# Four graph layers on one core: from layer-by-layer jobs to five lanes with a planned order for every engine

## The chip, the core and the metric

The kernel runs on one core of a Trainium2 chip. The metric is device microseconds (us) for one execution; a comparison runs both kernels in turns on the same chip. Engines are TensorE (PE; its weight loads are listed apart as PEld), VectorE (DVE), ScalarE (ACT), GpSimd (POOL) and SyncE (SP, which issues most loads and all stores).

## The reference, cut

```python
# x: (64, 256, 128) fp32, adj: (256, 256), 0/1; four layers, each with a residual and a layernorm
x = layernorm(x + L0(x, adj, ...))   # h = x@wo; e[i,k] = leaky(u1[idx1]+u2[idx2]) masked by adj;
                                     # softmax over i (the rows); out = att @ h + x @ wself
x = layernorm(x + L1(x, adj, ...))   # h = x@W; e[i,j] = leaky(h_i.a_src + h_j.a_dst) masked by adj + I;
                                     # softmax over j; elu(att @ h)
x = layernorm(x + L2(x, adj, ...))   # five gated steps:
                                     #   m = adj@h;  z, r = sigmoid(..m.. + u3 h);  v = tanh(..m.. + u5 (r*h))
                                     #   h = (1-z)*h + z*v
x = layernorm(x + L3(x, adj, ...))   # x W0 + adj x W1 + adj^2 x W2 + adj^3 x W3 (both halves share adj)
```

The graphs are independent. Both kernels work in 32 **units** of two graphs, 512 nodes of 128 features each.

## The kernel before

Everything is fp32. A unit's layer is a generator whose `yield`s cut it into pieces; four generators are live, and one piece of each is given out in turn. The program hands each engine its instructions as one list, so this turn-taking is the order of every engine's queue. The jobs are layer-major: all 32 units go through layer 0, then all through layer 1, and so on.

```python
    def run(jobs, width, gap):
        live, wait = [], 0
        while jobs or live:
            if jobs and len(live) < width and wait <= 0:
                live.append(jobs.pop(0))
                wait = gap
            wait -= 1
            live = [j for j in live if next(j, StopIteration) is not StopIteration]

    jobs = [layer(u) for layer in (layer0, layer1, layer2, layer3) for u in range(NU)]
    run(jobs, 4, 1)
```

Layer 1's attention has queries on partitions: mask added, leaky, maximum, exp with sums, then p is transposed for the product with h.

```python
    def layer1(u):
        ...
        for g in range(G):
            b, c = g // NC, g % NC
            nc.vector.scalar_tensor_tensor(e[:, b, c, :], ps_e[:, b * N : (b + 1) * N], es[:, g : g + 1], neg1[:, c, :],
                                           op0=ALU.add, op1=ALU.add)
        leaky(e, 0.2)
        nm = buf("nm", 4, [P, G])
        nc.vector.tensor_reduce(nm, e.rearrange("p b c j -> p (b c) j"), AX.X, ALU.max, negate=True)
        ...
            nc.scalar.activation(p[:, g // NC, g % NC, :], e[:, g // NC, g % NC, :], AF.Exp,
                                 bias=nm[:, g : g + 1], accum_out=s[:, g : g + 1])
        ...
                    nc.tensor.transpose(ps_t[:, jc, ic * P : (ic + 1) * P], p[:, b, ic, jc * P : (jc + 1) * P], ident)
            nc.vector.tensor_copy(pT[:, b], ps_t)
```

A normalisation takes four `bn_stats` and four `bn_aggr` a unit; layer 2 uses real sigmoids for r and z.

Of the kernel before, what the change touches and what calls it, by code (L numbers as in the profile page):

```python
# [8 lines left out]
F32 = mybir.dt.float32  # L9
AF = mybir.ActivationFunctionType  # L10
# [3 lines left out]
P = 128  # L14
NEG = -1.0e30
EPS = 1e-5
STEPS = 5


@with_exitstack  # L20
def kernel(
# [34 lines left out]
    G = UB * NC  # L56

    const = ctx.enter_context(tc.tile_pool(name="const", bufs=1))
    work = ctx.enter_context(tc.tile_pool(name="work", bufs=2))
    psum = ctx.enter_context(tc.tile_pool(name="psum", bufs=8, space=bass.MemoryType.PSUM))  # L60

    def bank(shape):
        return psum.tile(shape, F32, tag="ps", name="ps")


    def load(name, src, shape, eng=nc.gpsimd):
        t = const.tile(shape, F32, tag=name, name=name)
        eng.dma_start(t, src)
        return t
# [3 lines left out]
    X = []  # L73

    def load_x(u):
        X.append(load(f"x{u}", x_u[u], [P, UB, NC, D], nc.sync))

    load_x(0)
    adj_t = load("adj_t", adj.rearrange("(c p) j -> p c j", p=P), [P, NC, N], nc.sync)
    for u in range(1, NU):  # L80
        load_x(u)

    wo = load("wo", others_weight, [D, D])
    att = const.tile([D, 2], F32, tag="att", name="att")
    for k in range(2):
        nc.gpsimd.dma_start(att[:, k : k + 1], att_weight[k * D : (k + 1) * D, :])
    wself = load("wself", self_weight, [D, D])
    w1 = load("w1", W, [D, D])
    asd = const.tile([D, 2], F32, tag="asd", name="asd")
    nc.gpsimd.dma_start(asd[:, 0:1], a_src)  # L90
    nc.gpsimd.dma_start(asd[:, 1:2], a_dst)
    gates = [load(f"gate{k}", w, [D, 2, D]) for k, w in enumerate(
        w.rearrange("o (s d) -> o s d", s=2) for w in (w3_w, w4_w, w5_w))]
    u3 = load("u3", u3_w, [D, D])
    u5 = load("u5", u5_w, [D, D])
    biases = const.tile([D, 5], F32, tag="biases", name="biases")
    for k, b in enumerate((w3_b, w4_b, w5_b, u3_b, u5_b)):
        nc.gpsimd.dma_start(biases[:, k : k + 1], b.rearrange("(p o) -> p o", o=1))
    wk = load("wk", weight_1, [D, D, 7])


    ident = const.tile([P, P], F32, tag="ident", name="ident")
    make_identity(nc, ident)
    nhalf = const.tile([P, G], F32, tag="nhalf", name="nhalf")
    nc.vector.memset(nhalf, -0.5)

    def transposed(name, src):
        ps = bank([P, P])
        nc.tensor.transpose(ps, src, ident)
        t = const.tile([P, P], F32, tag=name, name=name)  # L110
        nc.vector.tensor_copy(t, ps)
        return t

    adjT = const.tile([P, NC, N], F32, tag="adjT", name="adjT")
    for mc in range(NC):
        ps = bank([P, N])
        for ic in range(NC):
            nc.tensor.transpose(ps[:, ic * P : (ic + 1) * P], adj_t[:, ic, mc * P : (mc + 1) * P], ident)
        nc.vector.tensor_copy(adjT[:, mc, :], ps)

    neg0 = const.tile([P, NC, N], F32, tag="neg0", name="neg0")
    nc.vector.tensor_scalar(neg0, adjT, 0.0, NEG, op0=ALU.is_le, op1=ALU.mult)
    neg1 = const.tile([P, NC, N], F32, tag="neg1", name="neg1")
    nc.vector.tensor_copy(neg1, adj_t)
    for c in range(NC):
        nc.vector.tensor_add(neg1[:, c, c * P : (c + 1) * P], adj_t[:, c, c * P : (c + 1) * P], ident)
    nc.vector.tensor_scalar(neg1, neg1, 0.0, NEG, op0=ALU.is_le, op1=ALU.mult)

    def projected(name, w, vecs):
        wT = transposed(name + "T", w)  # L130
        ps = bank([P, 2])
        nc.tensor.matmul(ps, wT, vecs, start=True, stop=True)
        t = const.tile([P, 2], F32, tag=name, name=name)
        nc.vector.tensor_copy(t, ps)
        return t

    wu = projected("wu", wo, att)
    wc = const.tile([P, 1], F32, tag="wc", name="wc")
    nc.vector.tensor_add(wc, wu[:, 0:1], wu[:, 1:2])
    wc_b = const.tile([P, P], F32, tag="wc_b", name="wc_b")  # L140
    nc.vector.tensor_copy(wc_b, wc.to_broadcast([P, P]))
    wsd = projected("wsd", w1, asd)
    wd_b = const.tile([P, P], F32, tag="wd_b", name="wd_b")
    nc.vector.tensor_copy(wd_b, wsd[:, 1:2].to_broadcast([P, P]))

    def layer2_weights():
        ws = []
        for k in range(3):
            ws.append(const.tile([D, D], F32, tag=f"gs{k}", name=f"gs{k}"))
            nc.vector.tensor_add(ws[k], gates[k][:, 0, :], gates[k][:, 1, :])  # L150

        nc.vector.tensor_sub(ws[0], ws[0], ws[1])
        wT = [transposed(f"gT{k}", ws[k]) for k in range(3)]
        bs = const.tile([D, 3], F32, tag="bs", name="bs")
        for k, j in enumerate((3, 3, 4)):
            nc.vector.tensor_add(bs[:, k : k + 1], biases[:, k : k + 1], biases[:, j : j + 1])
        return wT, transposed("u3T", u3), transposed("u5T", u5), bs

    def layer3_weights():

        w3 = const.tile([D, 2, 2, D], F32, tag="w3", name="w3")

        nc.vector.tensor_add(w3[:, 0, 0, :], wk[:, :, 0], ident)
        for k in range(1, 4):
            nc.vector.tensor_add(w3[:, k % 2, k // 2, :], wk[:, :, k], wk[:, :, k + 3])
        return w3

    def adj_squared():

        a2T = const.tile([P, NC, N], F32, tag="a2T", name="a2T")  # L170
        for mc in range(NC):
            ps = bank([P, N])
            for kc in range(NC):
                nc.tensor.matmul(ps, adj_t[:, kc, mc * P : (mc + 1) * P], adjT[:, kc, :],
                                 start=(kc == 0), stop=(kc == NC - 1))
            nc.vector.tensor_copy(a2T[:, mc, :], ps)
        return a2T

    (dT, wT4, wT5), u3T, u5T, bias2 = layer2_weights()
    w3 = layer3_weights()  # L180
    a2T = adj_squared()



    def buf(tag, bufs=2, shape=None):
        return work.tile(shape or [P, UB, NC, D], F32, tag=tag, name=tag, bufs=bufs)

    def feature_major(u):
        ps = bank([P, T])
        for g in range(G):  # L190
            nc.tensor.transpose(ps[:, g * P : (g + 1) * P], X[u][:, g // NC, g % NC, :], ident)
        xT = buf("xT", 6, [P, UB, N])
        nc.scalar.copy(xT.rearrange("p b n -> p (b n)"), ps)
        return xT

    def layernorm(u, y):

        st = buf("st", 4, [P, G, 6])
        mv = buf("mv", 4, [P, G, 2])
        for g in range(G):  # L200
            nc.vector.bn_stats(st[:, g, :], y[:, g, :])  # L201
        for g in range(G):
            nc.vector.bn_aggr(mv[:, g, :], st[:, g, :])
        ve = buf("ve", 4, [P, G])
        nc.vector.tensor_scalar_add(ve, mv[:, :, 1], EPS)  # L205
        rstd = buf("rstd", 4, [P, G])
        nc.gpsimd.tensor_tensor(rstd, ve, nhalf, op=ALU.pow)  # L207
        yield
        for g in range(G):
            nc.vector.tensor_scalar(X[u][:, g // NC, g % NC, :], y[:, g, :], mv[:, g, 0:1], rstd[:, g : g + 1],  # L210
                                    op0=ALU.subtract, op1=ALU.mult)

    def residual(u, other):

        y = buf("y", 4, [P, G, D])
        nc.vector.tensor_add(y, other, X[u].rearrange("p b c d -> p (b c) d"))
        return y

    def flat(t):
        return t.rearrange("p a b -> p (a b)")  # L220

    def leaky(e, slope):

        e = e.rearrange("p b c n -> p (b c n)")
        nc.vector.scalar_tensor_tensor(e, e, slope, e, op0=ALU.mult, op1=ALU.max)  # L225


    def layer0(u):
        xT = feature_major(u)
        yield  # L230
        ps_c = bank([P, T])
        nc.tensor.matmul(ps_c, wc_b, flat(xT), start=True, stop=True)
        ps_d = bank([P, UB])
        for b in range(UB):
            for k in range(2):
                nc.tensor.matmul(ps_d[:, b : b + 1], xT[:, b, k : N : 2], wu[:, k : k + 1],
                                 start=(k == 0), stop=(k == 1))
        ps_h = bank([P, G, D])
        for g in range(G):
            nc.tensor.matmul(ps_h[:, g, :], xT[:, g // NC, (g % NC) * P : (g % NC + 1) * P], wo,  # L240
                             start=True, stop=True)
        d = buf("d", 4, [P, UB])
        nc.vector.tensor_copy(d, ps_d)
        e = buf("e", 2, [P, UB, NC, N])
# [208 lines left out]
```

## Time and profile before

| | before |
|---|---|
| median of 3 runs | 2171.63 us (2171.27 to 2172.13) |
| profiled span, mean granted clock | 2168.6 us, 0.934 |
| TensorE, VectorE, ScalarE busy | 84%, 54%, 38% |

The page's busy shares are means over four layers with different limits. The prediction below shows the slices, the table of stages and the waits, and takes from the dense stretches what TensorE needs at full rate. One row that it names in words is this group (line, engine, operation, tiles, shapes, count; busy us and mean ns; idle before, and who ended it):

```profile
L365 DVE TENSOR_TENSOR t<-t,xT 128x512 f32<-128x512 f32 x160 | 110.3, 690 | 459.1 <-ACT t L363 459.1
```

VectorE waits there 459 us in all for layer 2's tanh. The prediction reads from it that the order of the queues, not the work in them, sets the pace of layer 2.

### The profile page before, as it was taken

The page shows a single profiled execution, that of the slowest core. Times are in us where ns is not written, and L with a number is a line of the kernel's source. Part 1 is how long each engine was busy: PE and PEld are TensorE (multiplying, and loading weights), DVE is VectorE, ACT ScalarE, POOL GpSimd, SP SyncE. Part 2 cuts the span into 40 slices and gives each one's busy share as a digit, 9 for nine tenths or more (in the row PEclk, how much of TensorE's full clock was granted, in tenths as well). Part 3 has the DMA queues.
Part 4 walks back from the last instruction along what each step waited for, and adds up shares of the span by engine and source line. Part 5 has one row for each costly group of instructions (what it writes and reads, how often), then busy time and mean ns, then how long its engine had stood idle before and what let it go on. Part 6 is the DMA issues. An engine that isn't in the chain of part 4 may idle for free.

```text
span 2168.6 us, 21458 instructions
## 1 busy us (share of the span) xinstructions
PE 1831.9 (84%) x7767; PEld 1247.7 (58%) x7767; DVE 1179.4 (54%) x3137; ACT 813.9 (38%) x1698; POOL 143.2 (7%) x152
## 2 busy tenths in 40 slices
PE   5888865556666998998998998998989989999998
PEld 4777754444444554555555555545545545568887
DVE  5988977777777535335335335354353353353333
ACT  1333333333333443443443443443434434433333
POOL 2111110000000000000000000000000000011111
PEclk9999977777777999999999999999999999999999
DMA  7000000000000000000000000000000000001111
GB/s 182 1 1 2 1 1 0 1 0 1 0 1 0 1 1 0 1 1 0 0 1 0 0 1 0 0 1 1 0 1 1 0 1 0 1 10 35 40 35 39
DMA packets 34842, 19.60 MB, mean 9 GB/s; under 512 B 1472, under 2 KB 34496, under 8 KB 34736
## 3 DMA queue, kind: packets, MB, share of 16 engines
q1 hardware_dynamic: 34064, 17.04, 2.9%
q8 instruction: 61, 1.00, 0.2%
q0 software_dynamic: 672, 1.19, 0.2%
q14 instruction: 45, 0.37, 0.1%
HBM read 9.84 MB, written 8.39 MB: 8 GB/s over the span
## 4 chain that ended last, share of the span: by engine, by line
PE 67%; DVE 20%; ACT 6%; POOL 3%; issue 2%; DMA 1%; POOLq 0%; ACTq 0%; DVEq 0%
PE ps L342 13%; PE ps L355 8%; PE ps L350 6%; PE ps L349 6%; PE ps L361 6%; PE ps L360 6%; PE ps L395 5%; ACT t L352 3%; PE ps L310 3%; DVE x L210 3%; DVE st L201 3%; POOL rstd L207 3%; PE ps L403 3%; PE ps L385 2%; DVE e L225 2%
## 5 line engine op out<-in xcount | busy, mean ns | idle before, releaser
L365 DVE TENSOR_TENSOR t<-t,xT 128x512 f32<-128x512 f32 x160 | 110.3, 690 | 459.1 <-ACT t L363 459.1
L342 PE MATMUL ps<-adjT,ht 128*128 128x256 f32 x1024 | 245.2, 382 | 25.8 <-ACT ht L375 25.8
L207 POOL TENSOR_TENSOR rstd<-ve,nhalf 128x4 f32<-128x4 f32 x128 | 132.7, 1037 | 2017.4 <-DVE ve L205 1881.1
L342 PEld LDWEIGHTS ps<-adjT,ht 128*128 128x128 f32 x1024 | 191.9, 190 | 99.2 <-ACT ht L375 56.4
L310 PE MATMUL ps<-ident,p 128*128 128x128 f32 x256 | 74.9, 422 | 166.0 <-ACT p L300 164.8
L355 PE MATMUL ps<-h,gT 128*128 128x512 f32 x320 | 180.1, 645 | 40.4 <-ACT t L352 40.4
L210 DVE TENSOR_SCALAR x<-y,mv,rstd 128x128 f32<-128x128 f32 x512 | 151.4, 344 | 92.7 <-POOL rstd L207 92.6
L354 DVE TENSOR_TENSOR y<-t,xT 128x512 f32<-128x512 f32 x160 | 110.0, 687 | 143.9 <-ACT t L352 143.9
L345 ACT COPY h<-ps 128x512 f32<-128x512 f32 x160 | 93.9, 587 | 225.9 <-PE ps L342 225.9
L201 DVE BATCH_NORM_STATS2 st<-y 128x6 f32<-128x128 f32 x512 | 115.9, 283 | 108.0 <-ACT y L407 107.2
L352 ACT ACTIVATE t<-ps,bs 128x512 f32<-128x512 f32 x160 | 110.0, 688 | 169.1 <-PE ps L350 169.1
L363 ACT ACTIVATE t<-ps,bs 128x512 f32<-128x512 f32 x160 | 110.1, 688 | 167.2 <-PE ps L361 167.2
L310 PEld LDWEIGHTS ps<-ident,p 128*128 128x128 f32 x256 | 48.7, 212 | 207.6 <-ACT p L300 180.9
L357 ACT ACTIVATE z<-ps,bs 128x512 f32<-128x512 f32 x160 | 110.0, 688 | 147.9 <-PE ps L355 147.9
L349 PE MATMUL ps<-xT,u3T 128*128 128x512 f32 x320 | 163.9, 594 | 0.0
L361 PE MATMUL ps<-y,u5T 128*128 128x512 f32 x320 | 163.5, 592 | 0.4 <-DVE y L354 0.4
L360 PE MATMUL ps<-h,gT 128*128 128x512 f32 x320 | 163.5, 592 | 0.0
L350 PE MATMUL ps<-h,gT 128*128 128x512 f32 x320 | 163.4, 592 | 0.0
L372 PEld LDWEIGHTS ps<-ident,xT 128*128 128x128 f32 x640 | 80.3, 144 | 112.5 <-issue 53.8
L372 PE MATMUL ps<-ident,xT 128*128 128x128 f32 x640 | 99.9, 280 | 35.5 <-DVE xT L368 35.5
L300 ACT ACTIVATE p<-e,nm 128x256 f32<-128x256 f32 x128 | 63.6, 499 | 161.0 <-DVE nm L296 161.0
L368 DVE TENSOR_TENSOR xT<-xT,t 128x512 f32<-128x512 f32 x160 | 110.5, 690 | 8.8
(124 smaller groups left out, 2954.5 us busy)
## 6 DMA issues: line engine op xcount, KB each, us to landing
x<-in_x_dram SPq DMA_DIRECT2D x32, 256.0 KB, 5.5
out_dram<-x SPq DMA_DIRECT2D x32, 256.0 KB, 2.3
wk<-in_L_gnn_weight_dram POOLq DMA_DIRECT2D x1, 448.0 KB, 6.6
gate<-in_L_gnn_w_w_dram POOLq DMA_DIRECT2D x3, 128.0 KB, 5.8
adj_t<-in_adj_dram SPq DMA_DIRECT2D x1, 256.0 KB, 3.2
u<-in_L_gnn_u_w_dram POOLq DMA_DIRECT2D x2, 64.0 KB, 5.9
wo<-L_gnn_others_weight_dram POOLq DMA_DIRECT2D x1, 64.0 KB, 3.4
wself<-n_L_gnn_self_weight_dram POOLq DMA_DIRECT2D x1, 64.0 KB, 5.2
```

Of the source, the lines that this page charges most:

```text
L201: nc.vector.bn_stats(st[:, g, :], y[:, g, :])
L207: nc.gpsimd.tensor_tensor(rstd, ve, nhalf, op=ALU.pow)
L210: nc.vector.tensor_scalar(X[u][:, g // NC, g % NC, :], y[:, g, :], mv[:, g, 0:1], rstd[:, g : g + 1], op0=ALU.subtract, op1=ALU.mult)
L310: nc.tensor.transpose(ps_t[:, jc, ic * P : (ic + 1) * P], p[:, b, ic, jc * P : (jc + 1) * P], ident)
L342: nc.tensor.matmul(ps_m[:, b, :], ht[:, b, mc, :], adjT[:, mc, :], start=(mc == 0), stop=(mc == NC - 1))
L349: nc.tensor.matmul(ps_r, u3T, hf, start=True, stop=False)
L350: nc.tensor.matmul(ps_r, wT4, mT, start=False, stop=True)
L352: nc.scalar.activation(r, ps_r, AF.Sigmoid, bias=bias2[:, 1:2])
L355: nc.tensor.matmul(ps_r, dT, mT, start=False, stop=True, skip_group_check=True)
L360: nc.tensor.matmul(ps_v, wT5, mT, start=True, stop=False)
L361: nc.tensor.matmul(ps_v, u5T, rh, start=False, stop=True)
L372: nc.tensor.transpose(ps_t[:, g, :], hT[:, g // NC, (g % NC) * P : (g % NC + 1) * P], ident)
```

## The change

Its intent is to keep TensorE full from start to end. Four things are new: (1) a **list plan**: the kernel is first written down as tasks with an engine, a cost in ns and the cells that they read and write; a plan then gives each engine its next ready task, oldest unit first, and fixes thereby the order of every queue and the use of the eight PSUM banks; (2) five **lanes**, each of which takes one unit through all four layers; (3) **layer 1's attention transposed**: keys on partitions, so no transposes of p, no maximum, the mask as a product, the row sums from a column of ones in h; (4) **paired statistics**: one `bn_stats` over two interleaved rows. Besides, sigmoids become tanh, layer 0's two weights (with the residual's identity) share one product, Prelu on ScalarE replaces VectorE's leaky passes, and all loads are issued by SyncE.

```diff
+LANES = 5
+LEAD = 20
+BANKS = 8
...
+class Plan:
+    LATENCY = {"pe": 220, "dve": 150, "act": 150, "pool": 200, "sp": 3000}
+    OWN = {"pe": 0, "dve": 70, "act": 70, "pool": 100, "sp": 0}
...
+    def seen_at(self, t, by):
+        return t.end if t.eng != by.eng else t.off + self.OWN[t.eng]
...
+            for e, tasks in ready.items():
+                if free[e] > now:
+                    continue
+                fit = [t for t in tasks if t.at <= now and len(t.takes) <= len(self.free_banks)]
+                if not fit:
+                    continue
+                t = min(fit, key=key)
...
+                free[e] = t.off = now + t.ns
+                t.end = t.off + self.LATENCY[e] + t.wait
...
 (layernorm)
-        for g in range(G):
-            nc.vector.bn_stats(st[:, g, :], y[:, g, :])
-        for g in range(G):
-            nc.vector.bn_aggr(mv[:, g, :], st[:, g, :])
+        for k, (c, view) in enumerate(pairs):
+            add(DVE, 330, lambda k=k, view=view: nc.vector.bn_stats(st.ap[:, k, :], view().rearrange("p j d -> p d j")),
+                (c,), (st,))
...
 (layer 1)
+            add(ACT, 400, lambda g=g, b=b: nc.scalar.activation(
+                e.ap[:, g, :], ps_e.ap[:, b * N : (b + 1) * N], AF.Prelu, bias=h.ap[:, g, D : D + 1], alpha=0.2),
+                (ps_e, h), (e,))
...
+        add(ACT, 950, lambda: nc.scalar.activation(ef, ef, AF.Exp), (e,), (e,))
+        add(DVE, 1150, lambda: nc.vector.tensor_mul(
+            p.ap.rearrange("p (b c) n -> p b (c n)", b=UB), e.ap.rearrange("p (b c) n -> p b (c n)", b=UB),
+            mask1.ap.rearrange("p (o c) n -> p o (c n)", o=1).to_broadcast([P, UB, NC * N])), (e, mask1), (p,))
...
 (layer 2)
-            nc.scalar.activation(r, ps_r, AF.Sigmoid, bias=bias2[:, 1:2])
+            add(ACT, 600, lambda ps_g=ps_g: nc.scalar.activation(r.ap, ps_g.ap, AF.Tanh, bias=bias2.ap[:, 1:2], scale=0.5),
+                (ps_g, bias2), (r,))
...
-    jobs = [layer(u) for layer in (layer0, layer1, layer2, layer3) for u in range(NU)]
-    run(jobs, 4, 1)
+    def spawn(u, lane):
+        for layer in (layer0, layer1, layer2, layer3):
+            layer(u, lanes[lane])
+
+    def first(t):
+        late = t.unit - (NU - LANES)
+        return (0, t.unit) if late < 0 else (1, t.step + late * LEAD)
+
+    with tc.manual_schedule():
+        for t in plan.run(spawn, range(NU), first):
+            t.fn()
```

LATENCY is the plan's **handover allowance**: how long after a task has left its engine another engine may count on its result; OWN is the same for the engine itself. `first` is the rule of what goes first: the oldest unit, and among the last five units the task with the fewest steps done, each unit LEAD (20) steps behind the one before.

## The prediction

> **What bounds the kernel now.** I read the page's busy shares first, then its forty slices, because a share over the whole span mixes stages.
>
> ```profile
> PE 1831.9 (84%) x7767; PEld 1247.7 (58%) x7767; DVE 1179.4 (54%) x3137; ACT 813.9 (38%) x1698; POOL 143.2 (7%) x152
> ...
> PE   5888865556666998998998998998989989999998
> ...
> DVE  5988977777777535335335335354353353353333
> ...
> PEclk9999977777777999999999999999999999999999
> ```
>
> The slices show four regimes. From slice 6 to slice 13 TensorE is 5 or 6 tenths busy, VectorE is at 7, and the granted clock sinks to 0.7; before and after that TensorE is at 8 or 9. The kernel runs layer after layer over all 32 units, so the regimes are the layers. From the TensorE timeline I took the times at which the first instructions of a new layer crowd out the last of the old (26, 262, 713 and 1928 us; the seams overlap by a few us) and asked for the busy time of each stretch. The columns are start:end, length, busy us and count of each engine, clock, share and rate of the DMA.
>
> ```profile
> 0.00:26.00 26.00, 4.81 (x18) 3.94 (x19) 7.36 (x31) 1.28 (x1) 10.46 (x24) 1.00 1.03 268
> 26.00:262.00 236.00, 204.17 (x1398) 177.03 (x1396) 208.08 (x664) 78.88 (x265) 28.52 (x28) 0.95 0.05 13
> 262.00:713.00 451.00, 276.81 (x1565) 229.90 (x1564) 349.31 (x910) 145.86 (x439) 35.15 (x34) 0.75 0.00 1
> 713.00:1928.00 1215.00, 1112.78 (x3654) 632.00 (x3653) 525.40 (x1105) 503.76 (x804) 35.76 (x33) 0.98 0.00 0
> 1928.00:2168.60 240.60, 233.28 (x1142) 204.82 (x1140) 89.27 (x430) 84.14 (x190) 33.27 (x33) 0.99 0.12 36
> ```
>
> So set-up takes 26 us, layer 0 236, layer 1 451, layer 2 1215, layer 3 241. Layer 1 is a chain and no full engine: its waits (who waited, for whom, us in total, times, longest) are those of the softmax, handed on from VectorE to ScalarE to TensorE.
>
> ```profile
> PEld ps L310 <- ACT p L300: 180.9, 62, 8.7
> PE ps L310 <- ACT p L300: 164.8, 31, 8.5
> ACT p L300 <- DVE nm L296: 161.0, 31, 6.2
> ```
>
> Layer 3 is the opposite; its chain of waits is TensorE alone, one unit in 7.35 us (the next 3.45 starts at 2008.92).
>
> ```profile
> 2001.57 3.45 PE ps L395 x16
> 2005.03 0.44 PE ps L191 x4
> 2005.46 1.73 PE ps L385 x8
> 2007.19 1.73 PE ps L403 x8
> ```
>
> **What TensorE needs.** That last view and the dense stretches of the timeline give its real price, from one start to the next: 0.86 us for a product of 512 columns (two instructions each), 1.73 for four of 256, 0.223 for one of 128, 0.44 for four transposes, 0.86 for the four one-column sums of layer 0. Per unit of before: layer 0 0.44+0.86+0.86+0.95+12 x 0.223 = 5.8; layer 1 0.44+0.86+4 x 0.45+0.90+8 x 0.223 = 5.8; layer 2 0.44+5 x (1.73+5 x 0.86+0.44) = 32.8; layer 3 7.35. Together 51.7 us, times 32 is 1654 us. The stages took 2169, so 515 us are lost, and I can say where: set-up 26, layer 0 236-185 = 51, layer 1 451-185 = 266, layer 2 1215-1049 = 166, layer 3 6. That is what a better order can hope for.
>
> **What the Trainium skill says.** "Perfetto Trace Analysis", section Optimization Strategy: where the most-contended engine changes over time, interleaving the regimes may help. The table of stages is such a kernel. "TensorE: Matmul & The Clock Gate", Part 1: the clock is granted at half or full rate by how busy the engine has been over windows of about 3.4 us. The trace agrees: in layer 1 the mean is 0.75, and two products of 128 columns with 0.45 us between starts at 71 us take 0.85 at 275 us, just after an idle of 2.84 us. The same page, under Engine queue depths: only weight loads may be pulled ahead, ScalarE and VectorE are strictly first in, first out. So a fixed order that is wrong makes every later instruction wait; layer 2 shows it, where VectorE sits 459 us before L365 for a tanh. "ScalarE: Activation LUTs", Table sets: a switch of set costs about 2.66 us, and tanh lies in the set of exp as well as in that of sigmoid. Before has two table loads in all, 1283 ns each, because its layers are apart; mixed layers with sigmoid would switch all the time.
>
> **The change, part by part.**
> - *The order.* Five lanes each take one unit through all four layers; a list plan with costs for each task fixes every queue. Its costs fit the trace: 1.667 ns a column and 5 ns make 858 ns for 512 columns (860 measured), 600 ns for a 512-column activation or VectorE operation (0.60 between starts in the chain, 0.69 as a row). Its handover allowances (150 to 220 ns after a task) are slightly long against the 0.2 us from a product's last slot to the activation behind it, so it should seldom promise data too early.
> - *Products.* Layer 0: the self weight with the identity added joins the other weight (four products of 256, 1.73), eight of 128 remain: 0.44+0.86+0.86+1.73+1.78 = 5.7. Layer 1: four of 129 columns (the score column rides along), one of 512, eight of 130, and no transposes of p: 0.44+0.90+0.86+1.81 = 4.0. Layers 2 and 3 as before. Sum 49.8 us, times 32 is **1594 us**: only 60 less than before. The rest of the gain must come out of the 515.
> - *VectorE.* Layer 1 loses the two passes over 1024 elements (leaky 1.22, maximum 1.21), the two copies of pT (1.38) and four sums with the mask (1.82), and gains one product with the mask (about 1.22); layer 0 loses leaky (1.22), half the maximum (0.6) and the residual sum (0.69). Statistics: 4 x 0.226 and 4 x 0.106 (busy over count) become two passes over 256 elements at perhaps 0.36 each: 0.6 saved, four times a unit. In all about 8.5 us a unit; before is 1179 us, so about 910 to 950.
> - *ScalarE.* Prelu takes over the leaky steps and one exp of 1024 replaces four with sums; it copies less. About 815 us again. Sigmoid becomes tanh of half the argument; with the factor folded in, it keeps three operations on VectorE after the gates.
>
> VectorE at some 58% and ScalarE at some 50% of 1600 us are beside TensorE; only TensorE's 1594 us lie on the path.
>
> **How full TensorE will be.** One pass of layer 2 as a chain is about 1.73+0.59+0.86+0.69+0.69+0.86+0.69+1.8+0.44+0.58 and 1 us of handovers, 10 us, of which TensorE works 6.47. A whole unit is, by the same adding, about 95 us of chain (layer 0 14, layer 1 16, layer 2 55, layer 3 10) against 49.8 of products. Five lanes give it 5 x 49.8 = 249 us to do 95 us of chain, so there is nearly always a product ready, and lanes in layers 0 and 1 put their VectorE work under the products of those in layer 2. I choose 3% for stalls where data come just too late for the weight load (48 us). To that: 9 us before the first work of layer 0 (the identity is now made at once instead of at 13.4 us, behind the loads); 12 us while all five lanes begin in VectorE's layers (13 us of VectorE against 9.7 of TensorE in layers 0 and 1 of each unit, with set-up between); 12 us at the end, where the last unit's statistics, power, scaling and store (some 6.5 us in before) have little beside them; 5 us for clock. 1594+48+9+12+12+5 = **1680 us**.
>
> **Rivals.**
> - *Wrong plan, strict queues.* Each unit has some 35 handovers into TensorE; if each cost 0.1 us, that is 112 us, and the time is about 1745. For it: oldest unit first means that data are used just as they come. Against: the costs match.
> - *Eight banks of PSUM.* Layer 0 holds two banks through its softmax and layer 3 two through its products. If they run out, lanes wait: 1750 to 1800. Against: layer 2, two thirds of the time, needs two or three a lane.
> - *VectorE as bound.* If strided passes and power handovers make it slower, it would have to grow from 930 to 1600 us; I do not believe it.
> - *Table loads.* If Prelu were not in the set of exp, switches of 1.28 us several times a unit would add over 150 us to ScalarE, still under TensorE, but stop the lanes: 1750 or more.
> - *Better than thought.* No stalls at all: about 1630.
>
> **Range and chances.** The floor is 1594 plus start and end, so I put the low end at 1640; the middle rivals give the high end, 1745. For within 2% of before, the stalls would have to eat nearly all 515 us: 0.02. Slower needs something unseen: 0.02. Faster: 0.96.
>
> **What would show it.** Right: no regimes in the slices, TensorE at 9 in nearly all from slice 2, clock 0.98 or more, VectorE 910 to 950 us, one or two table loads, the chain mostly TensorE. Wrong: clock under 0.95, waits of TensorE for VectorE or ScalarE over 80 us in total, many table loads, or a slow first or last tenth.

## The result, and the profile after

The changed kernel takes **1639.17 us** (median of 4 runs, 1638.58 to 1639.43) against 2171.45 us in the same rounds, a ratio of 0.7551 (95% interval 0.7538 to 0.7564). Here and below a ratio is the mean time of one kernel's fast runs over that of the other's in the same rounds, so it is not quite the ratio of the quoted medians. The predicted range began at 1640: the time lies just below it. The direction and most steps held; what failed is the size of one term, the stalls.

The page of the changed kernel, its busy shares and the slices that answer to those of before:

```profile
PE 1615.9 (99%) x6999; PEld 1095.2 (67%) x6999; DVE 950.4 (58%) x2214; ACT 820.2 (50%) x1602; POOL 145.7 (9%) x134
...
PE   8899999999999999999999999999999999999998
...
DVE  6844556655556655466555665555656556763544
...
PEclk9999999999999999999999999999999999999999
```

The regimes are gone: TensorE is at 9 tenths from slice 3 (the first is 1) to the last but one, VectorE is at 4 to 6 nearly throughout, and the clock never sinks (mean 0.999). The stretches (columns as in the prediction's table) show it in numbers:

```profile
20.00:60.00 40.00, 35.86 (x233) 29.35 (x233) 28.21 (x92) 25.84 (x74) 5.05 (x5) 1.00 0.53 126
...
400.00:800.00 400.00, 398.18 (x1739) 271.00 (x1738) 236.19 (x553) 203.57 (x405) 38.17 (x32) 1.00 0.02 6
800.00:1200.00 400.00, 398.50 (x1732) 269.80 (x1731) 231.39 (x537) 202.62 (x398) 37.42 (x32) 1.00 0.02 6
...
1600.00:1637.20 37.20, 30.07 (x138) 23.17 (x136) 17.60 (x49) 8.77 (x17) 6.04 (x6) 0.98 0.10 29
```

In the middle TensorE has a product under way for 398 of each 400 us. How the lanes interleave is seen in the TensorE timeline (start, length, engine, line, operation):

```profile
1006.03 0.49 PE L570 MATMUL ps<-ident,xT 128*128 128x128 f32 x3
1006.36 0.61 PE L504 MATMUL ps<-h,p 128*128 128x130 f32 x4
1006.81 0.61 PE L458 MATMUL ps<-h,p 128*128 128x128 f32 x4
1007.25 1.56 PE L527 MATMUL ps<-adjT,ht 128*128 128x256 f32 x6
```

L570 and L527 belong to layer 2, L504 to layer 1, L458 to layer 0, and there is no gap between them. TensorE's idle waits for a result of VectorE or ScalarE add up to 10.2 us in the whole run (14 and 10 waits); in before they were 314 us.

**Where the time is now.** TensorE's first product of layer 0's input starts at 9.2 us and its last product of all ends near 1630.0. The 1620.8 us between hold the 1594 us that the prediction worked out, 10.3 us of idle (21.3 in all, less 3.9 before 9.2 us and 7.1 after the last product), and 16.5 us left over, in which products lie further apart than their dense price though the busy row has no hole. The 16.5 are a remainder, so they are only as good as the 1594. A second count from the same trace gives each product that starts after 9.2 us the median time from one start to the next of its shape (429 ns for an instruction of 512 columns, of which a product has two, 216 for 256, 109 for 128; the one-column ones their mean of 99). So priced, the products need 1588 us and lie 33 us further apart than that: 9 us in the stretch up to 60 us, while the lanes fill, and 24 after it. Statistics, power, scaling and store of the last unit take the 7 us at the end.

### The profile page after: what moved, and what is told of

Read it like the earlier page. It is cut to its first block, busy times and chain, and to the rows that moved or that the text cites. A ratio compares the mean times of both kernels' runs of the same rounds, so it can differ in the third digit from the quotient of the medians.

```text
span 1637.2 us, 18751 instructions
## 1 busy us (share of the span) xinstructions
PE 1615.9 (99%) x6999; PEld 1095.2 (67%) x6999; DVE 950.4 (58%) x2214; ACT 820.2 (50%) x1602; POOL 145.7 (9%) x134
## 4 chain that ended last, share of the span: by engine, by line
PE 94%; DVE 3%; ACT 1%; POOL 0%; issue 0%; DMA 0%; POOLq 0%; DVEq 0%; ACTq 0%
PE ps L543 41%; PE ps L527 20%; PE ps L597 7%; PE ps L570 4%; PE ps L604 3%; PE ps L423 3%; PE ps L375 3%; PE ps L504 3%; PE ps L458 3%; PE ps L408 2%; PE ps L473 2%; PE ps L477 2%; PE ps L412 1%; DVE x L395 1%; DVE st L386 0%; POOL rstd L391 0%
## 5 line engine op out<-in xcount | busy, mean ns | idle before, releaser
L543 PE MATMUL ps<-m,gT 128*128 128x512 f32 x960 | 463.7, 595 | 1.0 <-ACT e L549 0.6
L543 PEld LDWEIGHTS ps<-m,gT 128*128 128x128 f32 x960 | 173.1, 190 | 135.3 <-issue 116.2
L527 PE MATMUL ps<-adjT,ht 128*128 128x256 f32 x1024 | 253.6, 381 | 0.5 <-ACT ht L574 0.5
L551 DVE SCALAR_TENSOR_TENSOR e<-e,xT 128x512 f32<-128x512 f32 x160 | 110.3, 690 | 205.0 <-ACT e L549 204.5
L527 PEld LDWEIGHTS ps<-adjT,ht 128*128 128x128 f32 x1024 | 188.1, 190 | 54.9 <-issue 27.4
L562 DVE TENSOR_TENSOR p<-p,xT 128x512 f32<-128x512 f32 x160 | 110.3, 689 | 175.8 <-ACT p L556 175.3
L558 ACT ACTIVATE e<-ps,bias 128x512 f32<-128x512 f32 x160 | 109.9, 687 | 146.6 <-PE ps L543 146.6
L543 PE MATMUL ps<-xT,gT 128*128 128x512 f32 x320 | 164.2, 595 | 0.5 <-ACT xT L377 0.5
L543 PE MATMUL ps<-e,u5T 128*128 128x512 f32 x320 | 163.0, 597 | 0.9 <-DVE e L551 0.8
L549 ACT ACTIVATE e<-ps,bias 128x512 f32<-128x512 f32 x160 | 109.9, 687 | 106.7 <-PE ps L543 106.0
L527 PE MATMUL ps<-adjT,x 128*128 128x256 f32 x512 | 143.6, 380 | 0.0
L570 PEld LDWEIGHTS ps<-ident,xT 128*128 128x128 f32 x640 | 83.7, 141 | 76.6 <-issue 53.4
L563 DVE SCALAR_TENSOR_TENSOR p<-e,p 128x512 f32<-128x512 f32 x160 | 110.2, 689 | 21.8 <-ACT e L558 18.7
L570 PE MATMUL ps<-ident,xT 128*128 128x128 f32 x640 | 118.7, 274 | 0.6 <-DVE xT L565 0.4
L395 DVE TENSOR_SCALAR x<-ps,st,rstd 128x128 f32<-128x128 f32 x256 | 93.4, 404 | 41.6 <-POOL rstd L391 41.0
L375 PE MATMUL ps<-ident,x 128*128 128x128 f32 x512 | 112.5, 276 | 1.6 <-DVE x L395 1.1
```

The lines of the kernel that those rows point to most:

```text
L375: add(PE, 110, lambda g=g: nc.tensor.transpose(ps.ap[:, g * P : (g + 1) * P], X[u].ap[:, g // NC, g % NC, :], ident.ap), (X[u], ident), (ps,))
L527: add(PE, mm_ns(N), lambda b=b, mc=mc: nc.tensor.matmul(ps.ap[:, b * N : (b + 1) * N], (src.ap if len(src.ap.shape) == 4 else src.ap.rearr ...
L543: add(PE, mm_ns(T), lambda: nc.tensor.matmul(ps.ap, w(), rhs.ap, start=start, stop=stop, skip_group_check=True), (c, rhs), (ps,))
L549: add(ACT, 600, lambda ps_g=ps_g: nc.scalar.activation(r.ap, ps_g.ap, AF.Tanh, bias=bias2.ap[:, 1:2], scale=0.5), (ps_g, bias2), (r,))
L551: add(DVE, 600, lambda h=h: nc.vector.scalar_tensor_tensor(r.ap, r.ap, 1.0, h.ap, op0=ALU.add, op1=ALU.mult), (r, h), (r,))
L562: add(DVE, 600, lambda h=h: nc.vector.tensor_sub(v.ap, v.ap, h.ap), (v, h), (v,))
```

## The experiments

What bothered me: I had put 48 us for data that come just too late, 12 for the filling of the lanes and 5 for the clock, 65 in all, and found 27 (10.3 idle and 16.5 left over), or 33 by the second count. I also had given the mixing of layers the first place. My theory after the result was "margin": the plan's allowances are long enough, so data are there when their turn comes. Its rivals were "slack" (with five lanes any order works), "mixing" (the layers of VectorE lie under layer 2), and "less work" (the attention and the statistics). Every kernel below gave correct results.

### e1 to e4: mixing, stagger, margin, work

**e1** keeps tasks, plan and lanes, but hands out jobs layer by layer:

```diff
-        for layer in (layer0, layer1, layer2, layer3):
-            layer(u, lanes[lane])
+        (layer0, layer1, layer2, layer3)[job // NU](job % NU, lanes[lane])
...
-        late = t.unit - (NU - LANES)
+        late = t.unit - (4 * NU - LANES)
...
-        for t in plan.run(spawn, range(NU), first):
+        for t in plan.run(spawn, range(4 * NU), first):
```

> The changed kernel with every task, cost and lane kept, but the list of jobs is layer by layer: a lane takes layer 0 of a unit, then layer 0 of another, and layer 1 of any unit starts after all of layer 0 has been given out. It tells the mixing of layers from the quality of the plan. If the mixing brings the time: layer 0 about 200 us (VectorE and TensorE near 180 each), layer 1 205 to 225 (VectorE 6.9 us a unit against 4.0 of products), layer 2 about 1065, layer 3 240, with start and end 1730 to 1760 us, and a clock below 0.95 in layer 1. If the plan alone keeps TensorE full: 1640 to 1660.

Measured: 1701.53 us, ratio 0.7836 (0.7823 to 0.7849). Neither expectation: the mixing is worth 62 us of 532, the rest 470. The stretches of e1:

```profile
9.00:400.00 391.00, 337.50 (x2156) 288.27 (x2155) 343.07 (x1030) 249.54 (x661) 73.23 (x60) 0.94 0.09 22
400.00:1450.00 1050.00, 1049.63 (x3672) 608.26 (x3671) 514.95 (x928) 507.35 (x803) 40.97 (x36) 1.00 0.00 1
```

Without any mixing but at the seams, layer 2 (nearly all of the second stretch) runs at 1050 us, its need of 1049, where before took 1215; by the second count the products of this stretch lose 7 us. So the 166 us lost in layer 2 came back without mixing. No run separates the planned order from the fifth lane and the tanh in this. What mixing repairs is the first stretch: layers 0 and 1 need 9.7 x 32 = 310 us and take 391, with VectorE at 88% and the clock at 0.94. I had expected 405 to 425 there.

**e2** changes only the rule of what goes first, from the oldest unit to the unit with the fewest steps done:

```diff
-        late = t.unit - (NU - LANES)
-        return (0, t.unit) if late < 0 else (1, t.step + late * LEAD)
+        return (-1, t.unit) if t.unit < 0 else (t.step, t.unit)
```

> The changed kernel with another rule for what goes first: the task with the fewest steps done in its unit, not the oldest unit. The five lanes then move through the layers side by side. If it is the stagger of the lanes that puts the VectorE layers under the products of layer 2, the time is 1700 to 1760 us. If five lanes of any order are enough: 1640 to 1660.

Measured: 1987.69 us, ratio 0.9158 (0.9144 to 0.9172), far worse than both numbers. The lanes reach the end of a unit together: the first products of layer 0 come in bursts of five units, every 303.8 us. TensorE is idle for 269 us until a result of VectorE or ScalarE is there, and the clock is lower (mean 0.926). The largest of its waits are these:

```profile
PE ps L375 <- DVE x L395: 157.6, 15, 17.2
PE ps L504 <- DVE p L491: 39.8, 8, 6.2
```

L375 transposes what the normalisation at L395 writes, at the start of a layer: I read it as all lanes at the seam of two layers, with nothing to cover the handover. Part of the loss is another effect, that 32 units in rounds of five leave two for the last round. The trace separates the two: a full round is 60.8 us a unit, and the last one takes 151 us for two units, 30 us over that. So some 318 of the 348 us that the same tasks, costs and lanes lose under another rule lie in the full rounds, and "any order of five lanes" is refuted.

**e3** sets the handover allowances to zero:

```diff
-    LATENCY = {"pe": 220, "dve": 150, "act": 150, "pool": 200, "sp": 3000}
-    OWN = {"pe": 0, "dve": 70, "act": 70, "pool": 100, "sp": 0}
+    LATENCY = {"pe": 0, "dve": 0, "act": 0, "pool": 0, "sp": 3000}
+    OWN = {"pe": 0, "dve": 0, "act": 0, "pool": 0, "sp": 0}
```

> The changed kernel with all handover allowances in the plan (220, 150, 70 ns and so on) set to zero, so that the plan believes each result is there at the instant the instruction has been issued and orders the strict queues accordingly. Theory 'margin' (stalls are rare because the plan never promises too early): some 35 handovers a unit are late by about 0.2 us each, 1700 to 1780 us. Theory 'slack' (what is next in order was mostly ready long before, so lateness does not reach TensorE): under 1660 us.

Measured: 1770.06 us, ratio 0.8155 (0.8143 to 0.8168), as "margin" had it. (The expectation's own numbers, 35 x 32 handovers at 0.2 us, make 224 us, more than its range; the measured 131 us are 0.12 us for each of these 1120.) The loss of 131 us hides well: TensorE is busy for 1697.6 of 1767.6 us, and its idle waits for VectorE and ScalarE are 49 us. It is plainer in the waits of the weight loads. In e3:

```profile
PEld ps L543 <- ACT e L549: 70.5, 101, 0.9
PEld ps L543 <- DVE e L551: 52.5, 109, 1.6
PEld ps L570 <- DVE xT L565: 47.4, 84, 1.2
PEld ps L543 <- ACT m L539: 45.1, 98, 0.7
```

and in the changed kernel as it is:

```profile
PEld ps L543 <- DVE e L551: 21.9, 56, 1.1
PEld ps L570 <- DVE xT L565: 14.2, 43, 0.6
PEld ps L543 <- ACT m L539: 7.3, 26, 0.7
PEld ps L543 <- ACT e L549: 2.9, 7, 0.8
```

Summed over all rows whose releaser is VectorE or ScalarE, weight loads waited 322 us in 636 waits in e3 and 85 us in 244 waits in the changed kernel. Not all of that is lost, since a load runs ahead of its product, but the order is clear. The rival that I had named "wrong plan, strict queues" at 1745 us is real; the changed kernel avoids it by its allowances.

**e4** makes the four one-column products of layer 0 twice, with the same result:

```diff
-        for b in range(UB):
+        for b in (0, 1, 0, 1):
```

> The changed kernel with the four one-column products of layer 0 made twice (the same result written again), 0.86 us more of TensorE a unit. If TensorE is the bound throughout, all of 32 x 0.86 = 27.5 us comes out: 1667 us. If there is idle time left to hide it: 1640 to 1650.

Measured: 1671.12 us, ratio 0.7698 (0.7687 to 0.7710): 32 us for 27.5 us of dense work. Nothing hides it. TensorE's work is the bound; the 4 us more may be the unhidden loads of these short products, which I did not test.

### e5 and e10: more margin

**e5** doubles the allowances of e3's first two lines, **e10** triples them (440 and 660 for TensorE, 300 and 450 for VectorE and ScalarE, and so on).

> The changed kernel with all handover allowances of the plan doubled (440, 300, 140 ns and so on). The run with none gave 1770 us. If the allowances as written leave part of the results still late, more margin helps: 1625 to 1636 us. If they are just long enough, doubling only makes the plan hold back products that are ready: 1640 to 1665 us.

Measured: 1627.92 us, ratio 0.7500 (0.7489 to 0.7511). This beats the changed kernel, whose interval begins at 0.7538. So the allowances as written still left part of the results late: the waits of weight loads for VectorE and ScalarE fall further, from 85 to 45 us in all. Two of the rows shown for e3, now in e5:

```profile
PEld ps L543 <- DVE e L551: 2.9, 10, 0.7
PEld ps L570 <- DVE xT L565: 2.7, 9, 0.5
```

> The changed kernel with three times the handover allowances (660, 450, 210 ns and so on). None gave 1770, as written 1639, double 1628. If there is still lateness to take away: 1620 to 1625 us. If double has used up the gain: 1627 to 1640 us.

Measured: 1633.30 us, ratio 0.7525 (0.7513 to 0.7536). These waits stay at 43 us, yet the time rises by 5 us. I read it as products held back, but no view shows it directly; TensorE's idle waits for VectorE and ScalarE are 11 us in place of 8. None, single, double, triple give 1770, 1639, 1628, 1633 us, and by the second count the products lie 163, 33, 21 and 28 us further apart than they need.

### e6, e7 and e14: costs and lanes

**e6** lets the plan believe that every task but loads and stores takes 300 ns:

```diff
+        if eng != "sp":
+            ns = 300
         t = Task(eng, ns, fn, self.unit, wait)
```

> The changed kernel with every task of the plan, except the loads and stores, costed at the same 300 ns, and the allowances kept. If a strict queue needs the plan to know the costs, the order is wrong nearly everywhere: 1720 us or more, TensorE idle 80 us or more. If five lanes and oldest first are enough whatever the costs: under 1670 us.

Measured: 1842.27 us, ratio 0.8494 (0.8479 to 0.8508). TensorE idles 153 us for VectorE and ScalarE, 87.4 us of them at the transposes of layer 2's new state (L572 here is L570 of the changed kernel, two lines lower):

```profile
PE ps L572 <- DVE xT L567: 87.4, 89, 2.1
```

The plan's costs are worth 203 us.

**e7** has three lanes, **e14** four:

```diff
-LANES = 5
+LANES = 3
```

> The changed kernel with three lanes in place of five, the plan made anew for them. One unit's chain was put at 95 us against 49.8 us of products, so three lanes have 149 us of products to cover 95 us and collide more often: 1680 to 1760 us with TensorE idle 40 us or more. If the number of lanes hardly matters once the plan is good: under 1655 us.

> The changed kernel with four lanes. Five gave 1639, three 1750. If each further lane halves what is lost against the need of TensorE (1594 and some 17 for start and end, so 28 lost with five and 139 with three): about 1670 to 1685 us. If four already cover the chain of a unit: under 1650 us.

Measured: 1750.14 us (ratio 0.8065, 0.8052 to 0.8079) with three and 1667.61 us (0.7680, 0.7669 to 0.7692) with four, 2 us under the range: the loss over 1611 us (need, start and end) goes from 139 to 57 to 28 us, slightly better than halving. TensorE's idle waits for VectorE and ScalarE are 80, 28 and 10 us with three, four and five lanes, and the loss by the second count 143, 61 and 33 us. So slack counts as well as margin: three lanes with the right allowances are about as bad as five with none. A sixth lane could not be run: with LANES = 6 the build stops, since the buffers ask for 215.19 KB of a partition and 207.87 are left.

### e8, e11, e13: the arithmetic

**e8** is the kernel before in its old order with the new attention of layer 1 alone:

```diff
-            nc.vector.scalar_tensor_tensor(e[:, b, c, :], ps_e[:, b * N : (b + 1) * N], es[:, g : g + 1], neg1[:, c, :],
-                                           op0=ALU.add, op1=ALU.add)
-        leaky(e, 0.2)
...
-        nc.vector.tensor_reduce(nm, e.rearrange("p b c j -> p (b c) j"), AX.X, ALU.max, negate=True)
...
+            nc.scalar.activation(e[:, b, c, :], ps_e[:, b * N : (b + 1) * N], AF.Prelu, bias=h[:, g, D : D + 1], alpha=0.2)
+        nc.scalar.activation(ef, ef, AF.Exp)
+        nc.vector.tensor_mul(p.rearrange("p b c n -> p b (c n)"), e.rearrange("p b c n -> p b (c n)"),
+                             mask1.rearrange("p (o c) n -> p o (c n)", o=1).to_broadcast([P, UB, NC * N]))
```

> The kernel before, in its old order, with only layer 1's attention made as in the change (scores with keys on partitions, no maximum, mask by a product, sums by a column of ones, no transposes). VectorE loses about 4.4 us of 11.7 a unit and TensorE 1.8 of 5.8. If layer 1 was bound by its VectorE passes its stage falls from 451 to 260 to 310 us, the whole to 1980 to 2040 us. If it was the strict order of four jobs in step, less than 80 us is gained: above 2090 us.

Measured: 2078.18 us, ratio 0.9575 (0.9561 to 0.9590): between the two expectations. Layer 1's stage falls from 451 to 358 us but stays a chain. Its waits and its stretch:

```profile
PE ps L308 <- DVE p L299: 146.1, 32, 5.1
```

```profile
262.00:620.00 358.00, 207.33 (x1051) 180.92 (x1050) 241.50 (x789) 156.09 (x343) 35.63 (x35) 0.80 0.00 1
```

TensorE waits 4.6 us per unit for the masked p, and the granted clock is low (0.80 in the mean): in the timeline the eight products after such a wait take 3.4 to 3.8 us, against 1.8 at full rate. So the new attention alone gives 93 us in the old order.

**e11** is the opposite: the changed kernel with the old attention written as tasks of the plan (mask added, leaky, maximum, four exps with sums, eight transposes, two copies).

> The changed kernel (five lanes, plan, allowances as written) with layer 1's attention made in the old way: mask added, leaky and maximum on VectorE, four exps with sums, p transposed on TensorE. TensorE gets 5.8 in place of 4.0 us a unit, VectorE about 4.4 us more. If TensorE's work bounds and VectorE's is hidden: 1639 + 57 = 1696, 1690 to 1710 us. If VectorE (then near 1090 us busy) and the longer chain come to the path: 1730 us or more.

Measured: 1711.49 us, ratio 0.7891 (0.7875 to 0.7907), 72 us more than the changed kernel and 1.5 over the range. TensorE's busy time rose by 63 us, which is about its 57 us of work; VectorE's rose by 117 us to 1067 and stayed beside it. The other 9 us are idle time of TensorE: its waits for VectorE and ScalarE go from 10.2 to 19.4 us.

**e13** undoes the paired statistics alone (four `bn_stats` and four `bn_aggr` again, in the plan).

> The changed kernel with the paired statistics alone undone: four passes over 128 elements and four aggregations for each normalisation in place of two interleaved passes over 256. VectorE busy rises by some 65 us (116 + 54 against 105) to about 1015, and the chain of a normalisation by about 0.5 us. If VectorE is beside TensorE: 1637 to 1648 us. If the lighter VectorE is a cause of the missing stalls: 1660 us or more.

Measured: 1646.12 us, ratio 0.7582 (0.7569 to 0.7595): 7 us more. The rows of the statistics add up to 192 us here against 105 in the changed kernel (they overlap in part: VectorE's busy time rises by 49 us, to 999), and all but 7 us of it is hidden. The largest rows of e13, then that of the changed kernel:

```profile
L389 DVE BATCH_NORM_STATS2 st<-ps 128x6 f32<-128x128 f32 x256 | 64.1, 286 | 93.7 <-PE ps L607 85.4 <-PE ps L461 6.2 <-PE ps L376 2.0
L392 DVE BATCH_NORM_AGGREGATE mv<-st 128x2 f32<-128x6 f32 x512 | 63.3, 160 | 0.0
```

```profile
L386 DVE BATCH_NORM_STATS2 st<-ps 128x6 f32<-128x256 f32 x128 | 54.1, 427 | 97.3 <-PE ps L604 91.6 <-PE ps L458 5.3 <-PE ps L375 0.2
```

### e12: the tanh

**e12** puts real sigmoids back into layer 2:

```diff
-            add(ACT, 600, lambda ps_g=ps_g: nc.scalar.activation(r.ap, ps_g.ap, AF.Tanh, bias=bias2.ap[:, 1:2], scale=0.5),
+            add(ACT, 600, lambda ps_g=ps_g: nc.scalar.activation(r.ap, ps_g.ap, AF.Sigmoid, bias=bias2.ap[:, 1:2]),
...
-            add(DVE, 600, lambda h=h: nc.vector.scalar_tensor_tensor(r.ap, r.ap, 1.0, h.ap, op0=ALU.add, op1=ALU.mult),
+            add(DVE, 600, lambda h=h: nc.vector.tensor_mul(r.ap, r.ap, h.ap),
```

> The changed kernel with real sigmoids in layer 2 in place of the tanh of half the argument. With lanes in different layers the set of tables must be changed each time exps and sigmoids alternate. If that is what the tanh is for: hundreds of table loads of 1.28 us on ScalarE and 1750 to 2300 us. If the sets overlap or the lanes rarely alternate: under 1660 us.

Measured: 1759.61 us, ratio 0.8108 (0.8094 to 0.8121). There are 160 table loads in place of one; the two largest groups:

```profile
L548 ACT ACT_TABLE_LOAD x55 | 70.6, 1283 | 1.0
L445 ACT ACT_TABLE_LOAD x38 | 48.8, 1283 | 0.6
```

ScalarE's busy time rises by 202 us to 1022, still far under TensorE's need, and yet 120 us come out: the plan knows nothing of the loads, and TensorE's idle waits for ScalarE go from 4 to 73 us. So with mixed layers, and a plan that leaves the loads out, the tanh is worth 120 us, twice what the mixing itself is worth (e1). A plan that counts the loads was not tried.

### e9: a version that beats both

**e9** takes e5 and lets VectorE form layer 0's weighted sum of even and odd nodes, so that two of four one-column products go:

```diff
...
+        add(DVE, 330, lambda: nc.vector.tensor_scalar_mul(tv, xb[:, :, 0:N:2], wu.ap[:, 0:1]), (xT, wu), (t,))
+        add(DVE, 330, lambda: nc.vector.scalar_tensor_tensor(tv, xb[:, :, 1:N:2], wu.ap[:, 1:2], tv, op0=ALU.mult,
+                                                             op1=ALU.add), (xT, wu, t), (t,))
...
-            for k in range(2):
-                tail.append(add(PE, 240, lambda b=b, k=k: nc.tensor.matmul(
-                    ps_d.ap[:, b : b + 1], xb[:, b, k : N : 2], wu.ap[:, k : k + 1], start=(k == 0), stop=(k == 1)),
...
+            add(PE, 240, lambda b=b: nc.tensor.matmul(
+                ps_d.ap[:, b : b + 1], tv[:, b, :], one.ap, start=True, stop=True), (t, one), (ps_d,))
```

> The changed kernel with doubled allowances (1628 us) and two of the four one-column products of layer 0 taken away: VectorE weighs the even and the odd nodes and adds them (two passes over 256 columns, some 0.8 us a unit), and one product with a column of ones per graph remains. If TensorE's work is all that bounds, half of the 32 us that doubling these products cost comes off: 1610 to 1616 us. If the added VectorE work delays layer 0 or its margin: 1624 us or more.

Measured: 1617.34 us, ratio 0.7450 (0.7439 to 0.7461), the best of all; against e5's 0.7500 (0.7489 to 0.7511) the intervals do not touch. It is 1.3 us outside the expected 1610 to 1616. The saving is 10.6 us of the 13.8 that two products cost at their dense price; TensorE's busy time fell by 11.6.

## Why the prediction was wrong, point by point

- **The need of TensorE (1594 us) was right.** The median prices give 1588, and e4 and e9 move it up and down and the time follows. Regimes gone, clock 0.999, ScalarE 820 (815), one table load, TensorE's waits 10 us (under 80): all as listed. VectorE's 950 at the edge of 910 to 950 is in part luck: the savings listed for it add up to 9.3 us a unit, not 8.5, which would leave 881. The list omits what was added, among others 22 us for the scaling passes, half of which now read PSUM (151 to 173 us) and 19 us for two new groups of small operations (L441, L444).
- **The step that failed is "I choose 3% for stalls where data come just too late for the weight load (48 us)".** In its place the run shows 24 us after the filling, by the second count. Its neighbours are not what failed: "12 us while all five lanes begin in VectorE's layers" measured 9 by the same count, the start 9.2 (9 predicted), the end about 7 (12), and "5 us for clock" lies within the 24, at a mean clock of 0.999. By the prediction's own price list, all three terms (65 us) come to 27, what is left of the span after 1594, 9 and 7. The 3% was chosen, not worked out. The runs show what moves the stalls: the allowances (e3, e5, e10: a loss of 163, 33, 21 and 28 us with none, single, double and triple), the lanes (e7, e14: 143, 61 and 33 with three, four and five) and the costs (e6).
- **"Slightly long" was wrong too, in the other direction.** The prediction took the allowances as slightly long, so that the plan "should seldom promise data too early". Yet weight loads waited 85 us for VectorE and ScalarE in 244 waits, and doubling the allowances took 40 of these away and 11 us off the time. So the stalls were half of what was forecast although the margin was too short. That five lanes cover most of the lateness is a reading of e7 and e14.
- **The range contradicted its own rivals.** The low end was put at 1640 with the words "the floor is 1594 plus start and end", but that sum is 1594 + 9 + 12 = 1615, and "no stalls at all" was given as about 1630. A low end at 1615 would have held 1639.17.
- **Mixing was overrated.** The prediction read the table of stages as a case for interleaving; e1 shows 62 of 532 us for it. The larger part is within the layers: layer 2's 166 lost us came back without mixing. How the rest splits is known only in part, since the shares depend on what else is there: the new attention is worth 93 us in the old order (e8) and 72 in the new one (e11), the paired statistics 7. The shared product of layer 0, Prelu in place of the leaky passes and the loads on SyncE were not tested alone.
- **Rivals.** A wrong plan costs what was feared (1770 in e3, 1842 in e6, against 1745), table loads too (e12, 1760 against "1750 or more"). VectorE is not the bound (e11, e13). Whether the eight PSUM banks ever held a lane back was not tested by a run; with 10 us of idle they can have cost little.

## What to carry to other kernels

Work out what the bounding engine needs from its dense stretches, and where queues are strict, plan their order from measured costs with handover allowances that err on the long side: here 0 to 2 times the allowance moved the time by 142 us, more than any part of the arithmetic that was tested. Give the engine enough independent chains (three, four, five lanes: 1750, 1668, 1639 us) and let the oldest go first, so that they spread out. And let the low end of a range be the sum of what cannot go away, not that sum with a cushion.

## What the Trainium skill lacked or had wrong

- "Perfetto Trace Analysis", Identifying the Most-Contended Engine, says that busy time of matmuls is a poor measure of the distance to roofline; the runs agree and give a size: in e3 TensorE is 96% busy over a span of 1768 us, though its products need 1594. The page does not say that late results show up as waits of weight loads (322 us in e3, 85 in the changed kernel, 45 in e5) rather than as idle TensorE.
- "TensorE: Matmul & The Clock Gate", Back-to-back issue gap, has no price for fp32 products (no page gives their time): here 860 ns for 512 columns, 223 for 128, 110 for a transpose in a row, from start to start at full clock.
- No page has the cost of the statistics: 0.43 us for 256 interleaved elements against 0.29 for 128, both read from PSUM, and 0.16 for an aggregation (rows of the changed kernel and of e13).
- "ScalarE: Activation LUTs", Table sets: its short list does not name Prelu; the changed kernel runs Prelu, exp, tanh and copies with one load.
- "ScalarE: Activation LUTs", What ACT_TABLE_LOAD costs: the 1283 ns of a load agree (160 loads in e12). The 2.66 us for a whole switch of set, which the prediction cites under Table sets, do not show. In e12 the time from the end of one activation over the load to the start of the next is 1.31 us in the median, and the one switch of before, at 716 us, takes the same.
- No page says what margin an order fixed beforehand wants: none, single, double, triple gave 1770, 1639, 1628 and 1633 us.
